# Two slots in one step of a fused attention and feed-forward loop: scores in one burst, values in one burst

## The chip, the cores and the metric

The kernel runs on one core of a Trainium2 chip. The metric is the device time of one execution in microseconds, the median of several runs. The core's engines are TensorE (PE in the profile; PEld are its weight loads), VectorE (DVE), ScalarE (ACT), GpSimd (POOL) and SyncE (SP), which here issues all the DMAs. Each engine works through its own instructions in order, and semaphores hold an instruction until what it needs is done.

## The reference

Four blocks follow one another, each `x = x + layernorm(block(layernorm(x)))` on an `x` of 4 x 512 tokens with 128 features: a linear attention, a stack of six layers (attention and feed-forward), a second attention with slopes, and a gated feed-forward. The change lies in the stack. One of its layers, cut to what matters:

```python
def local_attention(q, k, v):          # 16 heads of 64, windows of 32 queries
    ...
    bk2, bv2 = (look(bk), look(bv))    # each window sees itself and the one before: 64 keys
    sim = jnp.einsum('bhwie,bhwje->bhwij', bq, bk2) * QK_SCALE
    sim = jnp.where(mask, -jnp.finfo(sim.dtype).max, sim)
    attn = jax.nn.softmax(sim, -1)
    return jnp.einsum('bhwij,bhwje->bhwie', attn, bv2)

def attn_layer(x, Wqkv, qs, ksc, Wo):
    q, k, v = jnp.split(x @ Wqkv, 3, -1)
    q = l2norm(q) * qs
    k = l2norm(k) * ksc
    # rotary tables on q and k
    return local_attention(q, k, v) @ Wo

for i in range(DEPTH):
    x = attn_layer(shift_tokens(x), ...) + x
    x = ffn_layer(shift_tokens(x), ...) + x     # layernorm, W1, a * gelu(gate), W2
```

## The kernel before

The stack works on 48 units: six layers, four batches of 512 tokens, two halves of eight heads. A unit takes four **slots**, so there are 192 slots. A slot `n` is a pair of heads `p = n % 4` for the work on scores and values, and a block of 128 tokens `t = n % 4` for projections, transposes and values; the unit is `k = n // 4`. The loop at lines 733 to 750 goes slot by slot. In each step `s` it walks through the table `ORDER` (720 to 728) of pairs of a name and a number: the act of that name is written for slot `s + number`. A number as name is a part of the feed-forward, which is written when `s + number` is a multiple of 8, since a batch of one layer takes eight slots. The order is a manual schedule: nothing is moved later, and each engine runs its instructions in the order in which they were written.

The acts, by engine:

- TensorE: `p0` and `p1` (project, line 312) multiply tokens with the weights of q and k into a tile `pp`; `turn` (400) transposes four blocks of k into `tp`; `value` (430) makes `pv`; `score` (448 to 470) adds a mask and multiplies q and k; `weighted` (527 to 540) multiplies probabilities and values; `out` (554) projects into `py`. All but the bursts of `score` and `weighted` use the whole array of 128 x 128; the scores are made of tiles of 64 rows x 32 columns (eight mask records and 64 score records a slot), the values of 64 x 64 (64 records). A product of f32 shows two records.
- VectorE: `r0`, `r1` (323) multiply `pp` with the rotary tables into `t`; `q0`, `q1` (353) sum squares; `top` (472 to 479) takes the maximum of the scores; `inverse` (496), `by_key` (508, a transpose of probabilities, with four DMAs for `pT`), `flip` (410, a transpose of q).
- ScalarE: `s0`, `s1` (335) square `pp`; `kept` (404) copies `tp` into `kT`; `valued` (439) copies `pv` into `vn`, and after the fourth block three DMAs make the shifted copy `ve`; `e0`, `e1` (488) are four exponentials each with their sums; `attended` (546) copies the weighted values; `norms` works every fourth slot.
- GpSimd: `a0`, `a1` (347) add the two rotary products; `normed` (388), `normal` (501), `in` (524 and 525, four copies of quarters into `pT`), `refine`.
- SP: `place` (422) issues four DMAs for `qT`, and the DMAs named above.

The feed-forward's parts are 1 (adds `py` to the stream), 2 (transposes), 3 and 14 (statistics), 4, 5 (transposes back), 6 (first products and gelu), 8 and 7 (second products, multiplied on VectorE), 9 (last products), 15 (adds them); 10 to 13 end the last layer. In the slots of gelu two copies, `valued` and `attended`, are done by VectorE.

PSUM has eight banks: three tiles of one bank (`mm`) turn among all large products and transposes, one tile of two banks holds the scores, one tile of two banks the weighted values, one bank `py`. So a large product can start when one of the three banks has been left by its readers: `pp` by `r` and `s`, `tp` by `kept`, `pv` by `valued`. The score tile is free again when `e1` has read it.

## Time and profile before

| what | us |
| --- | --- |
| median of 3 runs | 1930.8 |
| lowest and highest | 1925.88 and 1931.06 |
| the profiled execution | 1923.8 |
| its span | 1922.0 |
| first part, until the loop's first projections | 92 |
| loop of the stack | about 92 to 1549 |
| second attention and last feed-forward | about 1549 to 1922 |

TensorE's granted clock is 0.97 over the span. The profile's lines name an engine, the source line, the operation, the tile written and those read, the shapes, and a count. In the order of time a line gives start and length in us. In the table of windows the columns are the window, its length, the busy time of PE, PEld, DVE, ACT and POOL with the instructions in brackets, the granted clock, the DMA share and GB/s. A wait names the engine and line that sat idle, what ended the idle time, the sum in us, the times and the longest.

### The profile page before, as it was taken

The page shows a single profiled execution, that of the slowest core. Times are in us where ns is not written, and L with a number is a line of the kernel's source. Part 1 is how long each engine was busy: PE and PEld are TensorE (multiplying, and loading weights), DVE is VectorE, ACT ScalarE, POOL GpSimd, SP SyncE. Part 2 cuts the span into 40 slices and gives each one's busy share as a digit, 9 for nine tenths or more (in the row PEclk, how much of TensorE's full clock was granted, in tenths as well). Part 3 has the DMA queues.
Part 4 walks back from the last instruction along what each step waited for, and adds up shares of the span by engine and source line. Part 5 has one row for each costly group of instructions (what it writes and reads, how often), then busy time and mean ns, then how long its engine had stood idle before and what let it go on. Part 6 is the DMA issues. An engine that isn't in the chain of part 4 may idle for free. (4 is left out here: it accounts for less than half of the span.)

```text
span 1922.0 us, 75651 instructions
## 1 busy us (share of the span) xinstructions
PE 1763.1 (92%) x30696; PEld 928.2 (48%) x30696; DVE 1590.5 (83%) x2552; ACT 1599.4 (83%) x4631; POOL 1512.9 (79%) x1969
## 2 busy tenths in 40 slices
PE   6779999999999999999999999999999876687876
PEld 3335555555555555555555555555555532233322
DVE  3698888888988899888899888998887468888864
ACT  4558888898888998888888889888998838799984
POOL 1289988898998889988899889998898528678850
PEclk8989999999999999999999999999999999898988
DMA  3024443334433444344443444433333310000000
GB/s 103 1 60 104 117 110 93 98 98 124 122 85 96 105 119 118 84 100 113 115 109 82 100 112 120 112 89 92 96 93 98 86 43 5 1 1 1 1 1 22
DMA packets 98893, 155.14 MB, mean 81 GB/s; under 512 B 29553, under 2 KB 57073, under 8 KB 93937
## 3 DMA queue, kind: packets, MB, share of 16 engines
q1 hardware_dynamic: 98544, 150.30, 30.7%
q8 instruction: 242, 3.96, 0.9%
q14 instruction: 107, 0.87, 0.2%
HBM read 23.31 MB, written 1.05 MB: 13 GB/s over the span
## 5 line engine op out<-in xcount | busy, mean ns | idle before, releaser
L69 ACT ACTIVATE pr<-sc,top,rn 128x64 f32<-128x64 f32 x1536 | 600.7, 406 | 71.0 <-PE pa L626 26.0
L347 POOL TENSOR_TENSOR r<-t 128x512 f32<-128x512 f32 x384 | 488.2, 1272 | 110.5 <-DVE t L323 103.0
L323 DVE TENSOR_TENSOR t<-pp,tab 128x1024 f32<-128x1024 f32 x384 | 467.3, 1218 | 25.7 <-PE pp L312 17.9
L312 PE MATMUL pp<-wqkv,z 128*128 128x512 f32 x768 | 409.2, 616 | 11.3 <-ACT sq L335 8.2
L335 ACT ACTIVATE sq<-pp 128x512 f32<-128x512 f32 x384 | 234.1, 610 | 100.6 <-DVE t L323 97.1
L69 ACT ACTIVATION_READ_ACCUMULATOR pr<-sc,top,rn 128x1 f32 x1536 | 316.1, 206 | 0.0
L353 DVE TENSOR_REDUCE ss<-sq 128x8 f32<-128x512 f32 x384 | 259.1, 675 | 0.6 <-ACT sq L335 0.5
L536 PEld LDWEIGHTS av<-pT,ve 64*64 64x64 f32 x6144 | 163.8, 134 | 154.4 <-PE py L554 79.6
L476 DVE TENSOR_REDUCE sc<-sc 128x8 f32<-128x512 f32 x192 | 132.6, 690 | 110.2 <-PE sc L465 108.0
L430 PE MATMUL pv<-wqkv,z 128*128 128x512 f32 x384 | 218.0, 650 | 5.7 <-ACT sq L335 5.7
L981 POOL TENSOR_TENSOR lb<-lb,la 128x2048 f32<-128x2048 f32 x39 | 177.6, 4554 | 54.7 <-ACT lb L69 41.0
L501 POOL TENSOR_TENSOR pr<-pr,den 128x512 f32<-128x512 f32 x192 | 200.3, 1043 | 21.2 <-DVE den L496 8.6
L536 PE MATMUL av<-pT,ve 64*64 64x32 f32 x6144 | 196.1, 222 | 8.5 <-DMA ve<-vn 5.7
L388 POOL TENSOR_TENSOR r<-r,rn 128x512 f32<-128x512 f32 x192 | 200.1, 1042 | 3.8
L312 PEld LDWEIGHTS pp<-wqkv,z 128*128 128x128 f32 x768 | 134.3, 191 | 141.4 <-issue 104.5
L554 PE MATMUL py<-attn,wo 128*128 128x512 f32 x384 | 197.6, 596 | 0.3 <-ACT attn L546 0.3
L536 PE MATMUL av<-pT,vn 64*64 64x32 f32 x6144 | 192.5, 219 | 0.0
L465 PE MATMUL sc<-kT,qT 64*32 64x64 f32 x12288 | 170.2, 223 | 3.1 <-issue 3.1
L524 POOL COPY pT<-blocks 32x256 f32<-32x256 f32 x384 | 149.7, 390 | 23.6 <-DVE blocks L508 7.2
L536 PEld LDWEIGHTS av<-pT,vn 64*64 64x64 f32 x6144 | 165.0, 135 | 0.1
L525 POOL COPY pT<-blocks 32x256 f32<-32x256 f32 x384 | 151.8, 395 | 16.1
L465 PEld LDWEIGHTS sc<-kT,qT 64*32 64x32 f32 x12288 | 155.0, 105 | 5.0 <-issue 4.0
(248 smaller groups left out, 3142.5 us busy)
## 6 DMA issues: line engine op xcount, KB each, us to landing
qT<-qb SPq DMA_DIRECT2D x768, 64.0 KB
ve<-vn SPq DMA_DIRECT2D x48, 768.0 KB
pT<-blocks SPq DMA_DIRECT2D x768, 32.0 KB
wqkv<-in_f_wqkv SPq DMA_DIRECT2D x36, 256.0 KB
ve<-vn SPq DMA_DIRECT2D x48, 192.0 KB
tab<-in_rot SPq DMA_DIRECT2D x12, 256.0 KB
wo<-in_f_wo SPq DMA_DIRECT2D x6, 512.0 KB
ve<-vn SPq DMA_DIRECT2D x48, 64.0 KB
```

Of the source, the lines that this page charges most:

```text
L69: done = nc.scalar.activation(out, in_, func, **kw)
L312: nc.tensor.matmul(pp, lhsT=z[b][:, WIN + t * P : WIN + (t + 1) * P], rhs=ws[i]["qkv", hf][:, m * S : (m + 1) * S], start=True, stop=True,)
L323: nc.vector.tensor_tensor(t12, o["pp", j].rearrange("p (h d) -> p h d", d=DH0).unsqueeze(1) .to_broadcast([P, 2, 8, DH0]), ws[i][f"tab{m}" ...
L335: nc.scalar.activation(sq, o["pp", j], AF.Square)
L347: nc.gpsimd.tensor_tensor(r, t1, t2[:, :, ::-1, :], ALU.add)
L353: nc.vector.tensor_reduce(o["ss"][:, m, t, :], o.pop(("sq", j)).rearrange("p (h d) -> p h d", d=DH0), AX.X, ALU.add,)
L388: nc.gpsimd.tensor_tensor(v, v, o["rn"][:, 1, t].unsqueeze(2).to_broadcast([P, 8, DH0]), ALU.mult)
L430: nc.tensor.matmul(pv, lhsT=z[b][:, WIN + t * P : WIN + (t + 1) * P], rhs=ws[i]["qkv", hf][:, 2 * S :], start=True, stop=True,)
L465: nc.tensor.matmul(scores[32 * w : 32 * w + 32, e, j, :], lhsT=o["qT"][rows, w, p, j, :], rhs=o["kT"][rows, p, q0 : q0 + KW], start=False, ...
L501: nc.gpsimd.tensor_tensor(pr, pr, o["den", p].unsqueeze(3).to_broadcast([P, 2, 4, KW]), ALU.mult)
L536: nc.tensor.matmul(av[64 * e : 64 * e + 64, h, 64 * j + 32 * c : 64 * j + 32 * c + 32], lhsT=vs[c][rows, j, (2 * p + e) * DH0 : (2 * p + e ...
L554: nc.tensor.matmul(ff["py"], lhsT=ws[i]["wo"][:, c, :], rhs=o.pop(("attn", p)), start=(c == 0), stop=(c == 7),)
```

## The change

The loop goes in steps of two slots. In a step the scores of both slots are written in one burst into one tile of the same two banks (now 2 heads x 2 slots x 4 x 64), first the masks of both, then the products of both. The weighted values of the two slots before are one burst too. All other acts stand twice in the new `ORDER`, once for each slot, at places of their own. The maximum is reduced into an SBUF tile (of three buffers) and multiplied there in place, where before it went through free columns of the score tile. Feed-forward parts have new places; those that don't fit the loop are written after it. The copies by VectorE in the slots of gelu are now `attended` and `valued` of the even slot of that step. The number of instructions of each act and the DMAs stay the same.

```diff
         def scored(n):
             k, p, o = of(n)
-            sc = o["raw", p] = scp.tile([P, 2, S], F32, tag="sc", name="sc")
-            scores = o["sc", p] = sc[:, :, 0 : 4 * KW].rearrange("p e (j k) -> p e j k", k=KW)
-            for w in range(4):
-                for e in range(2):
...
-            for j in range(4):
+            sc = scp.tile([P, 2, 2, 4, KW], F32, tag="sc", name="sc")
+            for u in range(2):
+                o["sc", p + u] = sc[:, :, u]
                 for w in range(4):
-                    q0 = j * P + w * WIN
                     for e in range(2):
                         rows = slice(64 * e, 64 * e + 64)
                         nc.tensor.matmul(
-                            scores[32 * w : 32 * w + 32, e, j, :],
...
+                            sc[32 * w : 32 * w + 32, e, u].rearrange("p j k -> p (j k)"),
+                            lhsT=identb[rows, 64 * e : 64 * e + 32], rhs=mask[rows, int(w == 0)],
+                            start=(u == 0), stop=False, skip_group_check=True,
                         )
+            for u in range(2):
+                for j in range(4):
+                    for w in range(4):
+                        q0 = j * P + w * WIN
+                        for e in range(2):
+                            rows = slice(64 * e, 64 * e + 64)
+                            nc.tensor.matmul(
+                                sc[32 * w : 32 * w + 32, e, u, j, :],
+                                lhsT=o["qT"][rows, w, p + u, j, :],
+                                rhs=o["kT"][rows, p + u, q0 : q0 + KW],
+                                start=False, stop=True, skip_group_check=True,
+                            )
 
         def topped(n):
             k, p, o = of(n)
-            sc = o.pop(("raw", p))
-            raw = sc[:, 0, 4 * KW : 4 * KW + 8].rearrange("p (e j) -> p e j", e=2)
-            nc.vector.tensor_reduce(raw, o["sc", p], AX.X, ALU.max, negate=True)
-            top = o["top", p] = work.tile([P, 2, 4], F32, name="top")
+            top = o["top", p] = work.tile([P, 2, 4], F32, bufs=3, name="top")
+            nc.vector.tensor_reduce(top, o["sc", p], AX.X, ALU.max, negate=True)
             rq = o["rn"][:, 0, :, 2 * p : 2 * p + 2]
-            nc.vector.tensor_tensor(top, raw, rq.rearrange("p j e -> p e j"), ALU.mult)
+            nc.vector.tensor_tensor(top, top, rq.rearrange("p j e -> p e j"), ALU.mult)
...
         def weighted(n):
             k, p, o = of(n)
-            vs, pT = o["vs"], o.pop(("pT", p))[0]
-            av = o["av", p] = avp.tile([P, 2, S], F32, name="av")
...
+            vs = o["vs"]
+            av = avp.tile([P, 2, 2, 4, 64], F32, name="av")
+            for u in range(2):
+                o["av", p + u] = av[:, :, u]
+                pT = o.pop(("pT", p + u))[0]
+                for j in range(4):
+                    for c in range(2):
+                        for h in range(2):
+                            rows = slice(64 * h, 64 * h + 64)
+                            for e in range(2):
+                                head = 2 * (p + u) + e
+                                nc.tensor.matmul(
+                                    av[64 * e : 64 * e + 64, h, u, j, 32 * c : 32 * c + 32],
+                                    lhsT=vs[c][rows, j, head * DH0 : (head + 1) * DH0],
+                                    rhs=pT[rows, c, 4 * e + j, :], start=True, stop=True,
+                                )
...
         ORDER = (
-            ("score", 0), (5, -6), ("top", 0), ("q1", 9), (8, -10), (7, -9), (2, -4), ("e0", 0),
-            ("p0", 10), ("turn", 4), (9, -13), ("place", 5), ("r0", 10), ("guard", 6), ("s0", 10),
-            ("a0", 10), ("by_key", -1), ("out", -4), (3, -4), ("in", -1), (15, -13), (1, -3),
-            ("e1", 0), ("kept", 4), (14, -4), ("p1", 10), ("r1", 10), ("q0", 10), ("weighted", -3),
-            (4, -5), (10, -14), ("inverse", 0), ("weights", 0), ("normal", 0), ("value", 2),
-            (11, -15), ("s1", 10), ("valued", 2), ("a1", 10), ("norms", 6), ("refine", 6),
-            (13, -17), ("attended", -3), ("normed", 6), (12, -16), (6, -7), ("flip", 9),
+            ("normed", 5), ("score", 0), ("q1", 9), (5, -6), (2, -4), ("in", -2), ("top", 0),
+            ("e0", 0), (7, -12), (8, -8), ("p0", 10), ("r0", 10), ("turn", 4), ("p1", 10),
+            ("kept", 4), ("weights", 1), ("by_key", -1), ("s0", 10), ("guard", 6), ("e1", 0),
+            (10, -14), ("r1", 10), ("out", -4), (11, -16), ("value", 2), ("valued", 2), ("a0", 10),
+            ("q0", 10), ("attended", -3), ("in", -1), ("s1", 10), ("a1", 10), ("top", 1),
+            ("place", 5), ("p0", 11), (12, -16), ("r0", 11), (3, -4), (9, -12), ("inverse", 0),
+            ("norms", 6), ("weights", 0), ("turn", 5), ("e0", 1), ("a0", 11), (14, -4), (15, -12),
+            ("flip", 9), ("s0", 11), ("normal", 0), ("place", 6), ("refine", 6), ("out", -3),
+            ("p1", 11), ("e1", 1), (4, -4), (1, -2), ("r1", 11), ("weighted", -2), (13, -16),
+            ("q0", 11), ("normed", 6), ("q1", 10), ("by_key", 0), ("kept", 5), ("inverse", 1),
+            ("s1", 11), ("a1", 11), ("normal", 1), ("attended", -2), ("value", 3), ("valued", 3),
+            ("flip", 10), (6, -6),
         )
-        AT = {what: n for what, n in ORDER}
+        STEP = 2
+        FIRST = max(n for what, n in ORDER if what == "p0")
+        ENDS = min(n for what, n in ORDER if not isinstance(what, int))
+        GELU = next(n for what, n in ORDER if what == 6)
...
-            for s in range(-AT["p0"], LAST + 4):
-                copy = nc.scalar.copy
-                if s % 8 == -AT[6] % 8 and -AT[6] < s:
-                    copy = nc.vector.tensor_copy
+            for s in range(-FIRST // STEP * STEP, LAST - ENDS, STEP):
                 for what, ahead in ORDER:
...
+                    n = s + ahead
...
+                        if n % 8 == 0:
+                            forward(n // 8, what)
+                    elif 0 <= n < LAST:
+                        copy = nc.scalar.copy
+                        if (s + GELU) % 8 == 0 and 0 < s + GELU and ahead % STEP == 0:
+                            copy = nc.vector.tensor_copy
...
+            for g in range(NB * DEPTH - 2, NB * DEPTH + 1):
+                for part in (1, 2, 3, 14, 4, 5, 6, 7, 8, 9, 15, 10, 11, 12, 13):
+                    forward(g, part)
```

`forward` keeps a set of the parts that are written, so that none is written twice, and leaves the same last parts to the next stage as before.

## The prediction

> **What bounds the kernel now.** I read the page first (engines and slices), then busy time by windows, then TensorE's records in order of time, then the waits, then ScalarE's order.
>
> ```profile
> PE 1763.1 (92%) x30696; PEld 928.2 (48%) x30696; DVE 1590.5 (83%) x2552; ACT 1599.4 (83%) x4631; POOL 1512.9 (79%) x1969
> ...
> PEclk8989999999999999999999999999999999898988
> ```
>
> ```profile
> 300.00:1400.00 1100.00, 1095.19 (x22466) 608.96 (x22464) 982.24 (x1702) 979.69 (x3356) 980.95 (x1435) 1.00 0.41 104
> ```
>
> From 300 to 1400 us TensorE is covered 1095 of 1100 us at clock 1.00, while VectorE, ScalarE and GpSimd are each at 89%. A busy TensorE is only a modelled one, so what counts is the time from record to record. One slot of the loop, TensorE alone (start, length, what):
>
> ```profile
> 804.18 1.02 PE L554 MATMUL py<-attn,wo 128*128 128x512 f32 x2
> 805.04 1.02 PE L312 MATMUL pp<-wqkv,z 128*128 128x512 f32 x2
> 806.00 0.32 PE L536 MATMUL av<-pT,ve 64*64 64x32 f32 x8
> ...
> 806.72 0.30 PE L536 MATMUL av<-pT,ve 64*64 64x32 f32 x8
> 806.83 0.30 PE L536 MATMUL av<-pT,vn 64*64 64x32 f32 x8
> 807.06 1.12 PE L430 MATMUL pv<-wqkv,z 128*128 128x512 f32 x2
> 808.12 0.30 PE L455 MATMUL sc<-mask,identb 64*32 64x256 bf16 x8
> 808.24 0.84 PE L465 MATMUL sc<-kT,qT 64*32 64x64 f32 x64
> 809.01 1.13 PE L312 MATMUL pp<-wqkv,z 128*128 128x512 f32 x2
> 809.97 0.60 PE L400 MATMUL tp<-ident,r 128*128 128x128 f32 x4
> ```
>
> The reader is to see that nothing stands idle, and that the borders cost. A product of two records takes 0.86 (804.18 to 805.04) between large ones, 0.96 ahead of a burst of small tiles (805.04), 0.96 behind one (809.01), 1.06 between two (807.06). Groups of eight value records start 0.12 apart, so the last, at 806.83, would give way at 806.95; the next product starts at 807.06, 0.11 later. One burst costs 0.10 + 0.11 + 0.10 = 0.31 us beside its records (the tail of a score burst put at the same 0.11).
>
> ```profile
> DVE sc L476 <- PE sc L465: 82.2, 102, 2.6
> ACT sq L335 <- DVE t L323: 62.3, 80, 1.4
> ...
> PEld pg L615 <- ACT kT L404: 15.5, 17, 1.0
> ```
>
> These are waits from 300 to 1400 us. No TensorE row waits long for another engine; the second says that ScalarE's square starts when VectorE's product has left the same PSUM tile; the third that a new tile waits for the copy that frees a bank.
>
> **What is removed.** 192 slots have two bursts each; two slots now share them: 2 x 96 bursts fewer, 192 x 0.31 = 59.5 us, or 2.5 us in a round of eight slots (the feed-forward's period; transposes L599 recur each 59.3 us, the mean of 17 rounds). The records themselves stay: 16 mask and 128 score records, 128 value records a step. TensorE's own need in a round, by the rows above: 8 x (0.12 + 0.77 + 0.96 + 0.43 + 0.86 + 0.96 + 1.06 + 1.06) = 49.8, 0.43 being the four transposes; for the feed-forward two groups of transposes at 0.49, nine products of 0.86 and 0.2 of borders: 58.7 in all, against 59.3 measured (0.6 of waits and layer ends, which I keep). After: 56.2. The other engines need 0.89 x 59.3 = 52.9, so none of them is a bound by its sum.
>
> **What is added: waits.** The score tile keeps its two banks and its one buffer, but holds two slots, side by side in the same bank. So the first mask record of a step waits until all four groups of exponentials of the step before are done, and the first maximum waits for the whole burst. I laid the new order out by hand on the four in-order engines. ScalarE's durations from these rows:
>
> ```profile
> 811.18 0.40 ACT L69 ACTIVATE pr<-sc,top,rn 128x64 f32<-128x64 f32 x1 [0.59 <-DVE top L479]
> ...
> 812.82 0.60 ACT L335 ACTIVATE sq<-pp 128x512 f32<-128x512 f32 x1
> 813.32 0.40 ACT L69 ACTIVATE pr<-sc,top,rn 128x64 f32<-128x64 f32 x1
> ...
> 814.84 0.60 ACT L404 COPY kT<-tp 128x512 f32<-128x512 f32 x1
> ```
>
> Four exponentials hold the engine 1.52 (813.32 to 814.84), a copy or square 0.5. The lead from scores to exponentials, early in the loop where VectorE isn't late:
>
> ```profile
> 138.43 0.85 PE L465 MATMUL sc<-kT,qT 64*32 64x64 f32 x64
> 139.31 0.70 DVE L476 TENSOR_REDUCE sc<-sc 128x8 f32<-128x512 f32 x1 [0.22 <-PE sc L465]
> 140.33 0.41 ACT L69 ACTIVATE pr<-sc,top,rn 128x64 f32<-128x64 f32 x1 [0.61 <-PE pp L312]
> ```
>
> The maximum starts 0.88 after the first of 64 records, the exponentials 1.02 later.
>
> A step without feed-forward work, from its first mask record at 0: 0.23 masks, 128 records to 1.5, maximum 1.75, exponentials e0 2.77, then on ScalarE kept 4.30, s0 4.77, e1 5.27, valued 6.80, attended 7.27, s1 7.75, e0 of the second slot 8.25, s0 9.78, e1 10.28 to 11.95. TensorE: p0 1.64, turn 2.6, p1 3.04, out 3.9, then value needs a bank. There are three for these products; I let each new tile take the one freed first. Value takes that freed by the k copy (4.9): 4.95, a wait of 0.15. The second p0 runs to 6.7; turn takes the bank of value, freed by valued at 7.4: 7.45, a wait of 0.75; out waits for attended to 7.92; p1 8.78, weighted 9.73 (2.0), value 11.73, next scores 12.8 against 11.8 without waits. The exponentials (11.95) don't decide there. Behind turn stand out, p1, both slots' values and the next scores; for them wait the maxima on VectorE and so ScalarE again, which closes the loop.
>
> The three other steps of a round, in the same way: with part 9 ahead of turn (2.6 us of products, which fill the hole) 0.2 of waits; with gelu 0.6, most of it its first product waiting for the second k copy; with part 8, 0.3. Sum 1.0 + 0.2 + 0.6 + 0.3 = 2.1. Round: 56.2 + 2.1 + 0.6 = 58.9 against 59.3, over 24 rounds 0.4 x 24 = 10 us gained. Bounds for the waits: zero (all 59.5 us stay), and 5.7 a round as in the third case below.
>
> Whether the shared bank truly makes engines take turns isn't shown: the row nearest is the square that waits for VectorE's product on one tile, 62.3 us in 80 waits. I take turns. If the maximum of the first slot could start after half the burst, 0.64 sooner, the step above would lose 0.64 of its 1.0 and the others some 0.6 together: 24 x 1.2 = 29 us more gain, 1891. The Trainium skill, page "PSUM — Partial Sum Buffer", section "PSUM bank collisions raise a hardware error", speaks against the change: accesses of two engines to one bank have to be ordered even at disjoint columns. By it the sum is the one that I take; no run here shows it yet.
>
> **Edits at nothing.** The maximum goes to SBUF in place of PSUM columns: reductions of this size with an SBUF result take 0.675 (L353) against 0.690, under 3 us over 192, in VectorE's 11% idle time, and at most 3 us either way without it. The number of DMAs is the same: per step eight for qT, eight for pT at about 0.6 us of SP's time each, 9.6 of some 14.7; the pT pieces are needed over half a step after their issue, those of ve at the end of a step some 9 us before the next but half step's values; covered unless a landing takes over 8 us. The chain shows 5.88 for ve at its worst, which is 0 to 3 us at the drain. GpSimd has 13.2 us a step of 14.7; after a refine step it is late by 3 us, and the products with part 9 give that back. Fill and drain have the same slots: nothing, from -5 to +5. After the loop parts 7, 9 and 15 of the last but one block stand alone: 0.86 + 2.6 us of products, ahead of the next stage's transposes; that stage begins with 4.95 of a DMA and 6.96 of VectorE work (1548.78 and 1553.83 in the chain), which hide them; up to 3.4 without. I take 0.
>
> The profiled execution took 1923.8 (span 1922.0), 7.0 under the median of 1930.8; with 10 off it would be 1913.8, and off the median 1921.
>
> **Rivals.**
> 1. Forecast, most is given back as waits: 1921, own range 1898 to 1945. Chance 0.42.
> 2. The waits hide: the kernel before has the same kind of bank waits and loses only 0.6 a round. Then 1930.8 - 59.5 = 1871. For it: 89% on the other engines leaves room. Against it: the hole ahead of turn is 0.75 with ScalarE never idle between. Chance 0.21.
> 3. Slower: banks are taken strictly in turn. Then the second slot's transposes wait not for valued (7.4) but for the first slot's second square (8.35), two copies further down ScalarE's queue: 0.9 more in each step, 3.6 a round, less the 0.4: 3.2 x 24 = 77, 2008; with a fifth of it absorbed where feed-forward products stand ahead, 1992. It decides as soon as the square ends later than TensorE's arrival at 6.7. For it: gelu's product waiting for the k copy (15.5 us, 17 times) fits strict turns too. Against: it fits the freed-first order as well, and a freed bank would lie idle. Chance 0.20.
> 4. The doubled burst runs slower than two: TensorE takes some 288 instructions in 1.6 us. Among the single bursts the 64 score records take from 0.63 to 1.62, a quarter over 0.70. At 0.15 to 0.5 a step this eats 14 to 48 us: 1935 to 1969. Chance 0.14.
> 5. The change doesn't make one burst of two, since the second slot's pT comes late and splits it: 1931 or a little more. Its pieces are issued half a step ahead. Chance 0.03.
>
> **Numbers.** A measurement of this kernel can tell 0.3%, 6 us, from no change. Faster: rival 2 and 0.29 of case 1: 0.50. Same: 0.07 of case 1, 0.03 of case 4: 0.10. Slower: the rest, 0.40. The range leaves out the best part of case 2 and the worst of case 3: 1876 to 1985.
>
> **What would show it.** Right: TensorE's share below 97% in the same windows; a new wait of tp (L400) for the value copy, some 0.7 us in two steps of four; 96 score bursts of 128 records with one border each; rounds of 58 to 59.5 us. Rival 2: rounds of 56 to 57 and no such wait. Rival 3: tp waits for the square, rounds over 61. Rival 4: 128 score records in over 1.45 us. I am wrong if the next scores wait for the exponentials, or VectorE, late by its order, sets the maxima.

## The result, and the profile after

The changed kernel takes 2098.99 us (median of 4 runs, 2096.93 to 2103.89) against 1928.34 for the kernel before in the same measurement: a ratio of 1.0888, 95% interval 1.0861 to 1.0916. It is 171 us slower. The profiled execution has a span of 2096.6 us against 1922.0.

From its page: busy time by engine, the granted clock by slices, the instruction queue, and the groups of the two bursts.

```profile
PE 1790.6 (85%) x30696; PEld 954.6 (46%) x30696; DVE 1644.9 (78%) x2552; ACT 1594.1 (76%) x4633; POOL 1515.9 (72%) x1969
...
PEclk9999999999999999999999999999999888988988
...
q8 instruction: 244, 4.00, 0.8%
...
L540 PE MATMUL av<-pT,ve 64*64 64x32 f32 x6144 | 206.7, 223 | 36.6 <-issue 15.9
...
L467 PE MATMUL sc<-kT,qT 64*32 64x64 f32 x12288 | 169.4, 230 | 51.7 <-issue 46.6
```

The number of TensorE's records is the same, 30696, but its share fell from 92% to 85%, and every other engine's fell with it: nothing is fuller than before, all wait more. The queue and the score group of the page before:

```profile
q8 instruction: 242, 3.96, 0.9%
...
L465 PE MATMUL sc<-kT,qT 64*32 64x64 f32 x12288 | 170.2, 223 | 3.1 <-issue 3.1
```

Before, the score products had 3.1 us of idle time ahead of them in the whole run; now it is 51.7, and 46.6 of that is "issue", time in which the engine waited for nothing that the profile shows. The same window as before says it for the loop (length, then PE, PEld, DVE, ACT, POOL, clock):

```profile
300.00:1400.00 1100.00, 997.50 (x20007) 563.08 (x20005) 920.14 (x1524) 875.77 (x3017) 881.85 (x1285) 0.98 0.38 94
```

TensorE is covered 997.5 of 1100 us, against 1095. A round of eight slots takes 66.3 us, against 59.3.

TensorE in order of time, one burst of values and one of scores of the kernel after (start, length, what; in brackets the idle time ahead):

```profile
800.98 0.63 PE L400 MATMUL tp<-ident,r 128*128 128x128 f32 x4 [0.63 <-ACT vn L439]
...
804.47 0.28 PE L540 MATMUL av<-pT,ve 64*64 64x32 f32 x2
805.07 0.25 PE L540 MATMUL av<-pT,ve 64*64 64x32 f32 x3 [0.32 <-issue]
...
805.89 1.13 PE L430 MATMUL pv<-wqkv,z 128*128 128x512 f32 x2
806.95 0.41 PE L456 MATMUL sc<-mask,identb 64*32 64x256 bf16 x16
807.18 0.86 PE L467 MATMUL sc<-kT,qT 64*32 64x64 f32 x63
809.28 0.86 PE L467 MATMUL sc<-kT,qT 64*32 64x64 f32 x65 [1.25 <-issue]
810.08 0.66 PE L580 MATMUL pt<-ident,z 128*128 128x128 f32 x4
```

Three things are to be seen. The transposes of `turn` wait 0.63 us for the value copy (800.98), as forecast. A border costs what it did: the product between the two bursts takes 1.06 (805.89 to 806.95). And the burst of 128 score records stops in its middle: 63 records, then 1.25 us of nothing, then 65.

Where the stage from the first score to the last value record got longer, from the start of one TensorE record to the start of the next (us):

| | before | after | difference |
| --- | --- | --- | --- |
| stage | 1417.4 | 1579.9 | +162.5 |
| inside the score bursts | 154.7 | 225.9 | +71.2 |
| inside the value bursts | 176.8 | 235.9 | +59.1 |
| everything else | 1085.9 | 1118.1 | +32.2 |
| from the last value record to the end | 378.5 | 390.6 | +12.1 |

In "everything else" the borders that went are worth -59.5 by the prediction's price, so the time between large products grew by 32.2 + 59.5 = 92 us, in waits and in slower products. So 130 us were lost inside the bursts, 92 outside them, 12 behind the loop, and 59.5 were won.

**The clock.** The window above has a granted clock of 0.98, where it was 1.00 before. The trace gives this clock as 1.0 or 0.5, in pieces of 3.4 us and multiples of it. In the stage of the table it was 0.5 for 82 us in the kernel after and for 10 us before. One such stretch of the kernel after (columns as in the window above; then TensorE in order of time):

```profile
341.00:347.70 6.70, 6.06 (x163) 4.27 (x164) 3.40 (x7) 1.77 (x3) 5.98 (x9) 0.50 0.31 75
```

```profile
341.64 0.32 PE L540 MATMUL av<-pT,ve 64*64 64x32 f32 x2 [1.70 <-issue]
...
342.21 2.07 PE L430 MATMUL pv<-wqkv,z 128*128 128x512 f32 x2
344.22 0.63 PE L456 MATMUL sc<-mask,identb 64*32 64x256 bf16 x16
```

The product at 342.21 takes 2.01 us until the next record starts, where the same one takes 1.06 at 805.89. Each of the 16 stretches follows 3.4 us in which TensorE stood idle for 1.0 to 2.7 us, here partly in a hole of a value burst. By estimate up to 36 us, half of the 72 us more at half clock, are a part of the 130 and 92. Since idle time precedes each stretch, the slow clock goes along with the holes and waits; that idle time sets it off wasn't tried by itself.

**The holes.** Count as a hole each gap of 0.15 us or more from the start of one record of a burst to the start of the next. Before there are 14 of them, 5.9 us in all; after, 136 with 118.2 us (73.1 in the score bursts, 45.1 in the value bursts), the median 0.81. The trace also has the packets of the queue that the page calls "instruction" (q8): 244 packets of 16384 bytes, each 1.1 us long in the median, and with 2 x 30696 records on TensorE that is one packet for 252 records, a product and its weight load being two. Of the 136 holes, 102 end between 1.05 and 1.62 us after such a packet has landed; packets as frequent as these would put 7% there by chance. In the lines above the packet ran from 806.65 to 807.79, and the scores went on at 809.28, 1.49 later. From the start of the packet to the end of the hole it takes 2.51 us in the median (2.26 to 2.84 for eight of ten), and a median of 1.61 us of that passes before TensorE runs dry. So TensorE's instructions come in pieces of some 250, and a piece's transfer starts about 2.5 us before it can be used; where small tiles use up what is left in less than that, the engine stands still.

VectorE and ScalarE behind that burst:

```profile
810.18 0.69 DVE L477 TENSOR_REDUCE top<-sc 128x8 f32<-128x512 f32 x1 [1.21 <-PE sc L467]
...
811.30 0.40 ACT L69 ACTIVATE pr<-sc,top,rn 128x64 f32<-128x64 f32 x1
```

The maximum of the first slot starts when the whole burst of both slots is done, and the exponentials 1.1 us later, so a hole in the score burst goes straight into ScalarE's queue. From the table of waits of the kernel after, 300 to 1400 us:

```profile
DVE top L477 <- PE sc L467: 126.8, 59, 5.7
PEld av L540 <- issue: 59.3, 58, 2.3
PEld tp L400 <- POOL pT L525: 50.3, 41, 2.0
...
PEld sc L467 <- issue: 40.6, 47, 2.7
```

The third row names GpSimd's `pT`, which had long been done. Of the 70 waits of `tp` over 0.25 us, 66 end 0.145 us after the end of a value copy (46 on ScalarE, 20 on VectorE): it is the bank of `pv`.

### The profile page after: what moved, and what is told of

Its sections match the earlier page's. It is cut to its first block, busy times and chain, and to the rows that moved or that the text cites. A ratio compares the mean times of both kernels' runs of the same rounds, so it can differ in the third digit from the quotient of the medians.

```text
span 2096.6 us, 75818 instructions
## 1 busy us (share of the span) xinstructions
PE 1790.6 (85%) x30696; PEld 954.6 (46%) x30696; DVE 1644.9 (78%) x2552; ACT 1594.1 (76%) x4633; POOL 1515.9 (72%) x1969
## 3 DMA queue, kind: packets, MB, share of 16 engines
HBM read 23.31 MB, written 1.05 MB: 12 GB/s over the span
## 4 chain that ended last, share of the span: by engine, by line
PE 47%; ACT 17%; DVE 16%; issue 8%; SPq 5%; DMA 5%; POOL 2%; DVEq 0%; POOLq 0%; ACTq 0%
PE av L540 8%; ACT pr L69 7%; PE sc L467 6%; PE pp L312 6%; PE pv L430 5%; DVE t L323 4%; PE pg L619 3%; ACT lb L69 3%; PE py L558 3%; PE py L640 3%; PE pa L630 3%; DVE la L991 3%; DVE lb L989 2%; DMA pT<-blocks 2%; PE tp L400 2%
## 5 line engine op out<-in xcount | busy, mean ns | idle before, releaser
L69 ACT ACTIVATE pr<-sc,top,rn 128x64 f32<-128x64 f32 x1536 | 606.6, 425 | 118.8 <-DVE top L479 63.5
L312 PE MATMUL pp<-wqkv,z 128*128 128x512 f32 x768 | 402.6, 608 | 11.2 <-ACT sq L335 6.8
L69 ACT ACTIVATION_READ_ACCUMULATOR pr<-sc,top,rn 128x1 f32 x1536 | 348.4, 227 | 0.0
L477 DVE TENSOR_REDUCE top<-sc 128x8 f32<-128x512 f32 x192 | 131.6, 685 | 202.0 <-PE sc L467 186.3
L335 ACT ACTIVATE sq<-pp 128x512 f32<-128x512 f32 x384 | 243.0, 633 | 54.4 <-DVE t L323 28.0
L353 DVE TENSOR_REDUCE ss<-sq 128x8 f32<-128x512 f32 x384 | 247.5, 665 | 0.2
L540 PE MATMUL av<-pT,ve 64*64 64x32 f32 x6144 | 206.7, 223 | 36.6 <-issue 15.9
L540 PEld LDWEIGHTS av<-pT,ve 64*64 64x64 f32 x6144 | 185.1, 137 | 109.3 <-issue 67.3
L540 PE MATMUL av<-pT,vn 64*64 64x32 f32 x6144 | 205.0, 223 | 14.6 <-issue 14.2
L467 PE MATMUL sc<-kT,qT 64*32 64x64 f32 x12288 | 169.4, 230 | 51.7 <-issue 46.6
L540 PEld LDWEIGHTS av<-pT,vn 64*64 64x64 f32 x6144 | 185.8, 138 | 20.4 <-issue 20.2
```

The source lines that it names most:

```text
L69: done = nc.scalar.activation(out, in_, func, **kw)
L312: nc.tensor.matmul(pp, lhsT=z[b][:, WIN + t * P : WIN + (t + 1) * P], rhs=ws[i]["qkv", hf][:, m * S : (m + 1) * S], start=True, stop=True,)
L335: nc.scalar.activation(sq, o["pp", j], AF.Square)
L353: nc.vector.tensor_reduce(o["ss"][:, m, t, :], o.pop(("sq", j)).rearrange("p (h d) -> p h d", d=DH0), AX.X, ALU.add,)
L467: nc.tensor.matmul(sc[32 * w : 32 * w + 32, e, u, j, :], lhsT=o["qT"][rows, w, p + u, j, :], rhs=o["kT"][rows, p + u, q0 : q0 + KW], start ...
L540: nc.tensor.matmul(av[64 * e : 64 * e + 64, h, u, j, 32 * c : 32 * c + 32], lhsT=vs[c][rows, j, head * DH0 : (head + 1) * DH0], rhs=pT[row ...
```

## The experiments

Two theories stood at the start: I, that TensorE's supply of instructions makes the holes and these make the loss; W, that the new order's waits between the engines make it and the holes come along. Ratios are to the kernel before of the same measurement (1926.6 to 1930.7 us), with 95% intervals. The last column is the time at half clock from the first score to the last value record; it and the holes are of one profiled execution each. Rows of `ORDER` in the edits are broken to fit.

| run | what it is | us | ratio | holes, us | half clock, us |
| --- | --- | --- | --- | --- | --- |
| before | | 1928.34 | 1 | 5.9 | 10 |
| after | | 2098.99 | 1.0888 (1.0861 to 1.0916) | 118.2 | 82 |
| e1 | after, bursts cut in two | 2219.01 | 1.1467 (1.1410 to 1.1524) | 5.2 | 195 |
| e5 | the same, scores ahead of the maximum | 2199.64 | 1.1394 (1.1326 to 1.1462) | 10.6 | 116 |
| e6 | after, bursts further apart | 2319.36 | 1.2014 (1.1941 to 1.2087) | 58.8 | 311 |
| e7 | after, only scores merged | 2203.99 | 1.1416 (1.1344 to 1.1489) | 42.4 | 219 |
| e8 | after, value copy earlier | 2169.61 | 1.1238 (1.1170 to 1.1306) | 118.8 | 85 |
| e9 | after, exponentials later | 2176.67 | 1.1276 (1.1243 to 1.1309) | 113.2 | 123 |
| e2 | after, half the records | 1980.90 | 1.0264 (1.0227 to 1.0301) | 59.2 | 55 |
| e3 | before, half the records | 1870.14 | 0.9690 (0.9657 to 0.9723) | 0 | 7 |
| e4 | before, single bursts side by side | 1986.01 | 1.0290 (1.0256 to 1.0325) | 50.7 | 17 |
| e10 | order of before, scores merged | 1993.51 | 1.0327 (1.0297 to 1.0357) | 34.6 | 14 |
| e11 | order of before, values merged | 1993.66 | 1.0328 (1.0298 to 1.0358) | 38.9 | 21 |
| e12 | order of before, both merged | 2117.32 | 1.0968 (1.0937 to 1.1000) | 77.0 | 41 |
| e13 | e12, half the records | 1956.58 | 1.0153 (1.0118 to 1.0188) | 19.6 | 31 |
| e14 | e10, half the records | 1946.47 | 1.0092 (1.0064 to 1.0121) | 1.4 | 14 |
| e15 | both merged, in one slot | 2307.49 | 1.1953 (1.1795 to 1.2111) | 82.8 | 143 |
| e16 | the same, transposes late | 2168.97 | 1.1252 (1.1217 to 1.1287) | 95.3 | 147 |
| e17 | before, transposes late | 1940.38 | 1.0076 (1.0053 to 1.0099) | 6.6 | 3 |

**e1: the bursts cut in two.** The second slot's score products become an act of their own, `score2`, and the values two acts.

```diff
-            ("e0", 0), (7, -12), (8, -8), ("p0", 10), ("r0", 10), ("turn", 4), ("p1", 10),
+            ("e0", 0), (7, -12), (8, -8), ("p0", 10), ("score2", 0), ("r0", 10), ("turn", 4), ("p1", 10),
...
-            ("out", -3), ("p1", 11), ("e1", 1), (4, -4), (1, -2), ("r1", 11), ("weighted", -2),
+            ("weighted", -2), ("out", -3), ("p1", 11), ("e1", 1), (4, -4), (1, -2), ("r1", 11), ("weighted2", -2),
```

> The changed kernel with its bursts halved again: the score products of the second slot stand behind the first large product (p0), the values of the first slot ahead of out; order, tiles and waits on banks are otherwise those of the changed kernel (2099.0 us). Theory I (instruction supply: the doubled bursts take 288 and 256 TensorE instructions faster than 16 KB pieces of code arrive; 111 us more of in-burst holes that end 1.05 to 1.6 us behind a piece's landing): holes inside bursts fall from 112 us to under 25, the four borders a step come back (+60), so 2030 to 2060. Theory W (the loss is in waits of the new order and the shared banks, and the holes only follow from them): the time stays or grows by the 60 of the borders, 2090 to 2160, and the holes move to other rows.

The holes went, from 118.2 to 5.2 us, as theory I has it, but the time rose by 120 us, and neither theory foresaw that. The order of time of e1 (first and second half of the scores, the maximum, the last exponential of four) and its longest wait of TensorE from 300 to 1500 us:

```profile
822.25 0.84 PE L472 MATMUL sc<-kT,qT 64*32 64x64 f32 x64
824.26 0.68 DVE L482 TENSOR_REDUCE top<-sc 128x8 f32<-128x512 f32 x1
...
826.60 0.40 ACT L69 ACTIVATE pr<-sc,top,rn 128x64 f32<-128x64 f32 x1
...
827.15 0.86 PE L472 MATMUL sc<-kT,qT 64*32 64x64 f32 x64 [2.61 <-DVE blocks L513]
```

```profile
PEld sc L472 <- ACT pr L69: 197.2, 67, 3.9
```

The second 64 products stood behind the first maximum and the first exponentials in the written order, and waited for both, though they write other columns: the two banks are shared, and in this program semaphores let the engines at them in the order written. So the turns that the prediction took are shown for this program; whether the chip needs them, as the page "PSUM — Partial Sum Buffer" of the Trainium skill has it ("PSUM bank collisions raise a hardware error"), no run here shows. The edit was therefore no clean test of the holes, and a part of its time is the clock, at half for 195 us.

**e5, e6, e7: the same without that flaw, and in parts.** In e5 `score2` stands ahead of `top`. In e6 the bursts stay whole, and the value burst moves ahead of `out` and `p1`. In e7 only the values are cut in two.

e5, against e1:

```diff
-            ("top", 0), ("e0", 0), (7, -12), (8, -8), ("p0", 10), ("score2", 0), ("r0", 10),
+            ("p0", 10), ("score2", 0), ("top", 0), ("e0", 0), (7, -12), (8, -8), ("r0", 10),
```

e6, against the kernel after (e7 has its `weighted` of one slot here, and `weighted2` at the old place):

```diff
-            ("out", -3), ("p1", 11), ("e1", 1), (4, -4), (1, -2), ("r1", 11), ("weighted", -2),
+            ("weighted", -2), ("out", -3), ("p1", 11), ("e1", 1), (4, -4), (1, -2), ("r1", 11),
```

> The kernel after, with both bursts cut in two again, without the flaw of e1_split: the second slot's 64 score products stand behind p0 but ahead of the first maximum in the order, the first slot's 64 value products ahead of out(-3). Theory I (TensorE's instructions come in pieces of 16384 bytes, 256 of them, and a burst uses them up faster than they are fetched): holes inside the bursts fall from some 120 us to under 30, borders come back (about +60), the first maximum starts some 1 us later in each step (0 to 40): 2040 to 2095. Theory B (engines may not use the shared banks in any order without long waits): the second slot's scores still wait, 2150 and more. Theory W (only waits between engines made the step long, the holes are a by-product): 2090 to 2150.

> The kernel after, nothing changed but that the value burst of 128 stands ahead of out(-3) and p1(11) instead of behind them: some 2.6 us of large products between it and the score burst instead of 0.9. Theory I: fewer instructions in the stretch of both bursts, so the holes fall from some 120 to between 60 and 100 us, most at the score records: 2035 to 2080. Theory W: holes are not set by the distance of bursts, and out(-3) and p1 wait as before: 2090 to 2120.

> The kernel after with the score burst of 128 whole and only the value burst cut in two, the first half ahead of out(-3). Theory I: the holes at the value records (some 47 us) fall under 15, those at the score records (some 70 us) stay between 40 and 75, and half of the borders come back (+30): 2055 to 2100. Theory W: borders only, +30: 2115 to 2145.

The holes fell about as the instruction supply says: to 10.6 in e5, to 37.3 at the scores and 5.0 at the values in e7, and to 58.8 in e6, though there most of the rest stands at the values (48.1) and not, as expected, at the scores (10.7, against 73.1 in the kernel after). The times missed theory I's ranges by 104 to 239 us and theory W's by 50 to 199; that of e5 lies in theory B's, but its second scores don't wait (1.7 us of idle time), so that isn't why. What waits in all three is the values: 90 to 112 us of idle time ahead of value records that isn't "issue", where it was 21 after. The waits of e6 from 300 to 1500 us show for what (the first row is the product behind the values):

```profile
PEld pv L430 <- ACT kT L404: 78.0, 48, 2.8
...
PE av L540 <- DMA pT<-blocks: 31.8, 21, 2.5
PE av L540 <- DMA ve<-vn: 19.9, 10, 2.3
```

A value burst that is two products, some 1.8 us, earlier comes before its transfers have landed. The cover that the prediction put at half a step isn't that thick in this order. The clock has a part too: at half for 311 us in e6 and 219 in e7, against 82, which by the same estimate is up to 114 and 68 us of the 220 and 105 by which they are slower than the kernel after.

**e8, e9: the bank that `turn` waits for.** e8 writes `out`, `value` and the value copy ahead of the first slot's second exponentials; e9 writes those exponentials behind the value copy and the attended copy.

The kernel after, e8 and e9:

```diff
-            ("guard", 6), ("e1", 0), (10, -14), ("r1", 10), ("out", -4), (11, -16), ("value", 2),
-            ("valued", 2), ("a0", 10), ("q0", 10), ("attended", -3), ("in", -1),
+            ("guard", 6), ("out", -4), ("value", 2), ("valued", 2), ("e1", 0), (10, -14), ("r1", 10),
+            (11, -16), ("a0", 10), ("q0", 10), ("attended", -3), ("in", -1),
```

```diff
+            ("guard", 6), (10, -14), ("r1", 10), ("out", -4), (11, -16), ("value", 2),
+            ("valued", 2), ("a0", 10), ("q0", 10), ("attended", -3), ("e1", 0), ("in", -1),
```

> The kernel after with out(-4), value(2) and its copy moved ahead of the second group of exponentials of the first slot, so that the bank that turn(5) needs is free 1.5 us earlier; bursts untouched. Theory W (the step's length is set by the wait of turn for the value copy, 43 us in all, and by what stands behind it): 2045 to 2075 with holes at 120 us as before. Theory I alone (waits move, the holes stay, TensorE arrives earlier and waits elsewhere): 2085 to 2110.

> The kernel after, only that the second group of exponentials of the first slot stands behind the value copy and the attended copy instead of ahead of them on ScalarE, so that the bank that turn(5) waits for is free some 1.5 us earlier and out(-3) is not later by more than 0.5. Theory W (the step is as long as turn's wait for the value copy makes it): the wait of 43 us falls under 15 and the time to 2045 to 2080. Theory I with a loop in which every engine hangs on the next (the wait moves to what hangs on those exponentials): 2090 to 2150.

In both the wait of `tp` went nearly as foreseen (TensorE's idle time ahead of `tp`: 39.2 us after, 8.3 in e8, 14.8 in e9), and in both the time rose, by 71 and 78 us, over the ranges of both theories. The waits of e8 from 300 to 1500 us:

```profile
PEld py L558 <- ACT attn L550: 52.8, 34, 1.6
...
PE py L558 <- ACT attn L550: 44.7, 34, 1.3
```

`out`, moved forward, waits for the attended copy; in e9 the next `p0` and `p1` wait instead (83.8 us of idle time ahead of `pp`, 11.2 after). In all five moves tried, e5 to e9, what was taken away at one place came back at another, and the time rose. The waits are real, but none of them stands alone.

**e2, e3, e4: records per time.** e2 and e3 make half as many score and value products, each over twice the columns, in the kernel after and before; every second block is so computed with its neighbour's weights. e4 changes only the order of before, so that the single bursts of values and scores follow each other.

e3 in the scores (the values and e2 likewise):

```diff
-            for j in range(4):
+            for j in (0, 2):
...
-                            rhs=o["kT"][rows, p, q0 : q0 + KW],
+                            rhs=o["kT"][rows, p, q0 : q0 + 2 * KW],
```

e4:

```diff
-            ("weighted", -3), (4, -5), (10, -14), ("inverse", 0), ("weights", 0), ("normal", 0), ("value", 2),
+            ("value", 2), ("weighted", -3), (4, -5), (10, -14), ("inverse", 0), ("weights", 0), ("normal", 0),
```

> The changed kernel with half as many score and value products, each over twice the columns (the columns and all tiles, waits and transfers stay; the scores and values of every second block are computed from the wrong block, so the output differs). Theory I: holes inside bursts under 15 us; the time falls by 111 and by what the shorter bursts free, 1880 to 1970. Theory W: the holes stay as waits, and the time falls by at most the shorter bursts, 30 to 60: 2040 to 2070.

> The kernel before with the same halving of the products (same columns, half the instructions, scores and values of every second block from the wrong block): the control for the halved changed kernel. If instruction supply is the whole loss of the change, the halved changed kernel is as fast as this one or faster by its 60 us of borders. If waits of the new order cost some 90 us besides, this one is 60 to 120 us faster than the halved changed kernel, at 1800 to 1870.

> The kernel before with value written ahead of weighted instead of behind it, so that the two bursts of a slot (128 and 144 instructions) stand next to each other with no large product between. Theory I: they now behave like one burst of 272 instructions in 2 us, and holes appear inside the bursts, 30 to 100 us in place of 6, for a border saved of 192 x 0.2 = 38: 1920 to 1990. Theory W: no more holes, 1885 to 1905.

The pages of e3 and of e4, the instruction queue and the score group of each:

```profile
q8 instruction: 146, 2.39, 0.6%
...
L465 PE MATMUL sc<-kT,qT 64*32 64x128 f32 x6144 | 130.5, 270 | 0.0
```

```profile
q8 instruction: 242, 3.96, 0.9%
...
L465 PE MATMUL sc<-kT,qT 64*32 64x64 f32 x12288 | 178.5, 223 | 41.1 <-issue 41.0
```

With half the records there are 146 packets in place of 242 and not one hole, over the same columns. With the same records as before and nothing merged, only side by side, the holes are there: 50.7 us, 36 of 44 with the end of a packet 1.05 to 1.62 us behind. That settles what makes them: instructions per time, not the size of a tile and not the merging as such. e4 also has its earlier `value` wait for its bank (24.7 us of idle time ahead of `pv`, 5.7 before), and saved borders; the sum is +58 us. e2 missed both theories: its time lies between their ranges, and it keeps 59.2 us of gaps where theory I gave under 15. Most of these are another thing: from 300 to 1400 us its bursts wait 45 us for transfers (`qT` 20.7, `pT` 12.1, `ve` 11.9).

**e10, e11, e12: the merged bursts without the new order.** These were the runs that decided. The order of before is kept line by line; at every even slot the scores of two slots are made, or at every odd slot the values of two, or both.

```diff
         def scored(n):
             k, p, o = of(n)
+            if p % 2:
+                return
...
         def weighted(n):
             k, p, o = of(n)
+            if p % 2:
+                return
```

(behind these lines the bodies of the kernel after)

> The kernel before, its order of one slot untouched, only that the scores of two slots are made in one burst at every even slot (96 bursts of 16 mask and 128 score records, the two slots side by side in the same two banks, as after). 96 borders go: -30 us. Theory I (instruction supply): a burst of 288 instructions meets holes, 30 to 75 us of them at the score records: 1925 to 1975. Theory W (the new order of two slots and its waits made the kernel slow, merged bursts cost nothing): 1890 to 1910.

> The kernel before, its order of one slot untouched, only that the values of two slots are made in one burst at every odd slot (96 bursts of 128 value records). 96 borders go: -30 us. Theory I: 256 instructions in some 1.7 us, so shorter holes than at the scores, 10 to 45 us: 1908 to 1945. Theory W: 1890 to 1910.

> The kernel before, its order of one slot untouched, with both bursts merged: scores of two slots at every even slot, values of two slots at every odd one. All 192 borders go, as in the change, but not the order. Theory I and W together (bursts cost holes, the order costs waits): -60 us of borders and 40 to 115 us of holes: 1910 to 1985, so 110 to 190 us faster than after. Theory W alone: 1865 to 1885. Theory I alone (the order costs nothing, the whole loss is in merged bursts): within 30 us of after, 2070 to 2130.

Each half alone costs 63 us, above the ranges of both theories, and both together 187, more than the change itself and in the range of theory I alone. So the loss isn't in the order of two slots: with the bursts merged that order is 18 us better than the old one (2098.99 against 2117.32). The holes are 34.6, 38.9 and 77.0 us, as many as theory I gave, and they look the same. e12 in order of time:

```profile
912.12 1.12 PE L430 MATMUL pv<-wqkv,z 128*128 128x512 f32 x2
913.17 0.41 PE L458 MATMUL sc<-mask,identb 64*32 64x256 bf16 x16
913.40 1.37 PE L469 MATMUL sc<-kT,qT 64*32 64x64 f32 x119
916.65 0.32 PE L469 MATMUL sc<-kT,qT 64*32 64x64 f32 x9 [1.88 <-issue]
```

The packet before the end of this hole ran from 914.29 to 915.24; the scores went on 1.41 later. But 77 us of holes less 59.5 of borders don't make 187. The length of a slot (from one product of `out` to the next, mean over 300 to 1400 us) shows the rest:

| kernel | one slot, us | the next, us | sum |
| --- | --- | --- | --- |
| before | 7.19 | 7.64 | 14.83 |
| e10, scores merged | 6.63 | 8.90 | 15.53 |
| e11, values merged | 6.60 | 8.86 | 15.46 |
| e12, both merged | 6.45 | 10.44 | 16.89 |

In e11 a slot gives its 64 value records and their border, 0.92 + 0.31, to its neighbour. The neighbour grows by 1.22, but the slot shrinks by only 0.59: TensorE, with a need of 58.7 in a round of 59.3 before, has no time to give away in the long slots and doesn't gain it all in the short ones. What holds the short ones isn't shown. The mean work of another engine, 0.89 x 59.3 / 8 = 6.6 us a slot, lies near their mean, but it is no floor: slot by slot in the round, the short ones of e11 take 8.22, 5.69, 6.78 and 5.66 us.

**e13, e14: merged bursts, half the records.** To part the holes from what else the doubled burst costs.

> e12_oneslot_both with half as many score and value products, each over twice the columns (every second block of scores and values is made with the weights of its neighbour, as in e3_before_half), to be set against e3_before_half at 1870. A merged burst then has no more instructions than a single one of the kernel before. If the waits that came with merged bursts are a consequence of the holes: 1840 to 1895. If the doubled burst itself makes them (both slots' scores stand in one pair of banks, so the first maximum waits for both, and TensorE's work is lumped): 1930 to 2010.

> e10_oneslot_scores (only the scores merged, order of before) with half as many score and value products, each over twice the columns, to be set against e3_before_half at 1870. Waits from holes: 1855 to 1885. Waits from the doubled burst itself: 1900 to 1945 (e10 lost 63 us to before).

| | full records | half the records |
| --- | --- | --- |
| single bursts, old order | 1930.63 | 1870.14 |
| both merged, old order | 2117.32, +187 | 1956.58, +86 |
| both merged, new order (after) | 2098.99, +171 | 1980.90, +111 |

With half the records merging still costs 86 to 111 us, what was expected if the doubled burst itself makes waits (e14, at +76, is 1.5 us over that range). So in the old order the doubled scores alone make 76 of the 86. Waits of e13 from 300 to 1400 us, two of TensorE and one of ScalarE, then ScalarE's of e3:

```profile
PE pp L312 <- ACT kT L404: 48.3, 54, 0.9
PE pv L430 <- ACT sq L335: 25.5, 53, 0.8
...
ACT pr L69 <- DVE top L481: 52.4, 85, 1.7
```

```profile
ACT pr L69 <- DVE top L479: 2.4, 4, 0.6
```

In e3 neither wait of TensorE is there. The exponentials wait for a maximum, the copies and squares of ScalarE come later, and TensorE's large products wait for the banks that these free. That the maximum, which waits for both slots' scores, starts this chain fits, but it wasn't tried by itself.

The gaps left in the bursts are 19.6 and 59.2 us, and few of them follow a packet (11 of 36, and 21 of 76). In the old order 100 us of the 187 go with the records (57 of them holes that are seen), in the new one 60 of the 171. So both causes are real, and neither is the whole. How sharp the split is stays open: half the records also take work from TensorE, so the others stand nearer to the bound; a part of the 111 is the clock (55 us at half in e2, 7 in e3); and e1 and e5, nearly without holes, were slower still.

**e15, e16, e17: does the place of the doubled bursts matter?** In e12 the doubled values stand one product ahead of the doubled scores. e15 makes the scores of an odd slot and the even one behind it, so that both bursts are in the odd slot, 5 us apart; for that k is transposed a slot earlier. e16 writes these transposes at the slot's end; e17 is its control, nothing merged.

The transposes of e15, and of e16 and e17:

```diff
-            ("p0", 10), ("turn", 4), (9, -13), ("place", 5), ("r0", 10), ("guard", 6), ("s0", 10),
+            ("p0", 10), ("turn", 5), (9, -13), ("place", 5), ("r0", 10), ("guard", 6), ("s0", 10),
...
-            ("e1", 0), ("kept", 4), (14, -4), ("p1", 10), ("r1", 10), ("q0", 10), ("weighted", -3),
+            ("e1", 0), ("kept", 5), (14, -4), ("p1", 10), ("r1", 10), ("q0", 10), ("weighted", -3),
```

```diff
+            ("normal", 0), ("value", 2), ("turn", 5), (11, -15), ("s1", 10), ("valued", 2), ("a1", 10),
+            ("kept", 5), ("norms", 6), ("refine", 6),
```

> The kernel before with both bursts merged as in e12_oneslot_both, but both in the odd slots, the score burst at the slot's start and the value burst some 5 us later, with none in the even slots (scores are made of an odd slot and the even one behind it, so k is transposed one slot earlier). In e12 the value burst of an odd slot is followed after one product by the score burst of the even one. Holes (instruction supply): fewer with the bursts apart, 30 to 60 us instead of 88. If the distance of the bursts is what lumps the slots: waits fall to 40 to 110 us from 221 and the time to 1900 to 1985. If any merged burst lumps a pair of slots, wherever it stands: 2040 to 2130, and the slots alternate with at least 2 us between them.

> e15_same_slot with k's transposes behind the value product at the end of the slot, so that they don't wait for GpSimd: both doubled bursts in the odd slots, some 5 us apart, none in the even ones. To be set against its control e17. If the distance of the bursts is what lumps the slots: within 40 us of e17, 1900 to 1985. If any merged burst costs, wherever it stands: 80 to 200 us above e17, and holes at the score records of 40 us and more in either case (288 instructions in 1.6 us).

> The kernel before with k's transposes one slot earlier, behind the value product at the slot's end, and their copy behind the value copy; nothing merged. The control of e16: the same need of TensorE as before, 1925 to 1960, more if the copies late in ScalarE's slot hold the banks of the next products.

e15 is over both its ranges and tells little: its transposes wait 205 us for GpSimd's `r`. e17 lies in its range, and e16 is 229 us above it, more than either theory gave, so the distance alone doesn't save the merged bursts; but e16 has waits of its own (78.7 us ahead of its masks for the exponentials that free the score banks, 54.3 for `qT`) and is no clean test of it. The place does matter to the holes: with no score burst near, 128 value records in one go meet almost none (median 1.86 us, twice the 0.92 of 64, and 182.2 us in all against 176.8 before), while its bursts of 144 score records still meet some: 39 of its 101 holes follow a packet, and a part of the rest is the wait for `qT`, since these scores span two units.

## Why the prediction was wrong

1. **The border's price held where it can be seen:** the product between two bursts still takes 1.06. The 59.5 us in all can't be measured apart from the losses.
2. **"The records themselves stay" is the step that failed.** Their number stays; their time rose by 130 us (71 at the scores, 59 at the values). The prediction carried the rate of the single burst into one twice as long. It had the mechanism at hand as its rival 4, TensorE's 288 instructions in 1.6 us, and gave it 14 to 48 us and a chance of 0.14, from the spread among the single bursts. Those rows could hardly show it: there each 144 instructions of scores had large products on either side. One burst does: the prediction gives their range as 0.63 to 1.62 us, but the one at 942 us takes 2.75, with a hole of 2.08 that ends 1.60 after a packet. In the kernel after, the 128 score records take 2.03 us from first to last in the median, where twice a single burst is 1.26. The test named for rival 4, over 1.45 us, came out on its side.
   The Trainium skill, page "Runtime: NRT & Kernel Launch", section "Instruction fetch mechanics", says that code comes in blocks of 16 KiB, 256 instructions, and that crossing into the next is mostly hidden. The packets of this trace have that size. Mostly hidden it was before (5.9 us of holes), where the two bursts of a slot and the product between them, 276 instructions, take 3.0 us (806.00 to 809.01), and not after (118.2), nor in e4, where 272 follow each other in some 1.9 us. So the measurement bounds the rule.
3. **The waits had a right place and half the size.** Forecast were 2.1 us a round, 24 x 2.1 = 50 us; measured are 92 outside the bursts, a part of it products at half clock, which the prediction, reading a clock of 1.00, had not in its sum. `turn` waits for the value copy, as laid out, 66 times where half of 96 steps were forecast. The layout ran on a burst without holes, with the first maximum 1.75 us after the first mask record; a hole puts it later. How much of the 92 comes of that wasn't tried by itself.
4. **The sum over a round hid what a doubled burst costs.** The prediction compared TensorE's need with the others' over a round of eight slots, 56.2 against 52.9, and took from that that none of them is a bound. The doubled scores cost 76 us (e14) even with half the records and in the old order: the exponentials wait for the maximum and TensorE for ScalarE's copies (48.3 us at `pp` in e13, none in e3). The prediction had such a chain in its layout, but put all its waits at 2.1 us a round. Work that moves from a slot to its neighbour lengthens the one by all of it and shortens the other by half (e11). Which of the two makes how much of the 86 to 111 us stays open.
5. **The shared banks** were right for this program: e1 shows that other columns of the same banks don't help. Rival 3, banks in strict turn, is out: `tp` waits for the value copy, not for the square.
6. **The round** takes 66.3 us, not 58 to 59.5; TensorE's share in the window is 90.7%, under 97% as foreseen.
7. **Edits at nothing.** The stretch behind the last value record grew by 12.1 us, where up to 3.4 was allowed for the parts written behind the loop, and 0 taken; which part it is wasn't tried. The cover of `pT` and `ve` nearly held in this order (18 us of idle time for them in the whole run, 0 to 3 allowed), and e6 shows that some 1.8 us less does not.

The blame also fell on the wrong part: the prediction saw the gain eaten by the waits of the new order, and e12 shows the loss without that order, at 41 us of half clock.

## What to carry to other kernels

Before small tiles are packed into longer bursts, count instructions, not columns: in these runs 272 to 288 TensorE instructions (products and weight loads each count) in 1.5 to 1.9 us made the engine stop (e4, e10), while 276 in 3.0 us with a large product between (before), and 256 in 1.9 us with only large products around (e16), hardly did. When one engine is nearly full and the others are not far behind, work moved from one slot to its neighbour can lengthen the one by all of it and shorten the other by less; lay out the waits slot by slot, not over the round. Read the granted clock beside every time: here stretches at half clock followed the idle time of the engine. And do a change's parts in the old order first: that one run (e12) told more than six reorderings of the new one.

## What the runs showed of the hardware

- TensorE's code arrives in packets of 16384 bytes of 1.1 us each. From the start of a packet to the first instruction that had waited for it passed 2.51 us in the median after, 2.61 in e4 and 2.54 in e12, almost the same whatever the kernel. At its start a median of 78 products, with their weight loads 156 instructions, were still to be run before the stop (after), so the transfer starts less than one packet ahead.
- Such a stop is "issue" in the profile, without a releaser, and is easily taken for a loss of the profile itself; only the packets of q8 beside it tell what it is.
- 64 score records over 64 columns took 0.63 us from first to last, and 32 over 128 columns 0.37 (e3): the time goes nearly by records, not by columns, here.
- TensorE's granted clock fell to 0.5 in pieces of 3.4 us. Each of the 16 stretches in the loop of the kernel after followed 3.4 us with 1.0 to 2.7 us of idle time of TensorE, each of the 49 in e6 followed 1.3 to 3.4; in them a product of 512 columns and two records took 2.01 us in place of 1.06.
- Writes of TensorE to banks of which VectorE and ScalarE still had other columns to read were held by semaphores until they were done: up to 3.9 us, 197 us in all in 67 waits (e1, 300 to 1500 us).
